# The first keys before the first norm's transposes, the first values after the first queries, and statistics next to their use, in a two-layer attention kernel

## The chip, the cores and the metric

The kernel runs on one core of a Trainium2 chip. The metric is the device time of one execution in microseconds (us); the number that counts is the median of several executions. A profile shows one of them.

A core has several engines with an instruction stream each: PE (TensorE, matmuls; "PEld" is its weight load), DVE (VectorE), ACT (ScalarE) and POOL (GpSimd). Each engine takes its instructions strictly in order, and waits where one needs a result of another engine. Transfers are started from a queue of an engine; this kernel starts nearly all of them from SP (SyncE), which does nothing else. SBUF is the memory that the engines work in; PSUM holds what matmuls write.

## The reference, cut to what matters

x has 32 sequences of 64 tokens with 512 features, and the context has the same shape. Everything is float32. Two layers follow one another; in each an attention onto the context and a feed-forward part are added to x.

```python
# layer 0
h = layernorm(x)
q = rope(h @ wq)                       # 32 heads of 128
k, v = rope(ctx @ wk), ctx @ wv        # 8 heads, each shared by 4 query heads
s = (q @ k.T) / sqrt(128)              # 64 x 64 per sequence and head
s = where(mask1 == 0, -1e9, s)         # a mask per sequence
x = x + softmax(s) @ v @ wo
x = x + swiglu_with_dequantized_weights(layernorm(x))

# layer 1
h = layernorm(x)
q, k = rmsnorm(h @ wq), rmsnorm(ctx @ wk)   # per head
v = ctx @ wv
x = x + softmax(q @ k.T / sqrt(128) + mask0) @ v @ wo   # one mask for all
x = x + memory_ffn_with_top_k(x)
```

The lines above are the order of the computation with the names shortened; the change touches the attention parts and their loads alone.

## The kernel before, in words

The 2048 tokens are worked in four chunks (`c` = 0 to 3) of 512, that is eight sequences or four tiles of 128 tokens. The attention of a layer runs over steps `(g, c)`: for each of the eight key heads `g`, the four chunks. All of x stays in SBUF (`x_sb[c]`), and so does its normed and transposed form (`xnT[c]`), which every head of the layer uses. So each chunk is normed only once per layer: chunk 0 ahead of the first step, the others during the steps of head 0.

One norm has two functions. `norm_stats` (L251) takes the statistics of the four tiles on DVE (`bn_stats` L258, `bn_aggr` L259), adds epsilon to all four variances at once (`ve`, in the profile `vea`, L262) and takes the power −1/2 on POOL (`rsa`, L247). `norm_apply` (L266) makes for each tile `xn` on DVE (L272, `xna` in the profile), transposes it by four matmuls with the identity into PSUM (L277, `xta`), and copies that to `xnT` on ACT (L281). The letter behind the names is the norm: a is layer 0's attention norm, c and d are later ones.

Queries and outputs are products of 512 by 512 that are computed as seven block products of eight matmuls (`quarters` L199, `product` L189) in place of eight. Each needs sums of blocks of both factors: `left_sums` (L163, four adds L166 to L169) on the first factor and `right_sums` (L171, four POOL adds L174 to L177) on the second. For the queries the first factor is the weight `wq` and the second `xnT`; for the output the first is the attention result `oT` and the second `wo`. The products are taken in the order P1, P2, P5, P6, P3, P7, P4; P1 and P2 use plain blocks, P5 the first sum of both sides.

A step consists of:

- `project_k` (L355, matmuls `pk` L363) and in layer 0 `rotate` (L405): ACT swaps halves (L410), DVE multiplies by cos (L412) and sin (L413), POOL adds into `kT` (L414). In layer 1 the keys are squared and summed for the norm instead.
- `project_q` (L416): the seven products; four times a "quarter" of the queries is finished by DVE (L427) and in layer 0 rotated like the keys, the last step again the POOL add (L414, `qT`).
- `norms` (L459, layer 1 alone): the sums of squares go through small matmuls (`pm` L471, L478), DVE (`qs` L484) and a power on POOL (`qr`, L247).
- `scores` (L488, matmuls `S` L496) into one PSUM buffer, and `softmax` (L505): `copy_predicated` of the mask on DVE (L519), maximum (L556), subtraction (L569), exp on ACT (L571), reciprocal (L574), multiplication on POOL (L577). DVE spreads maxima and sums by L301.
- `project_v` (L386, `pv` L395), `values` (L585, `po` L597, copied to `oT` on ACT L605, then left sums of `oT` on POOL) and the output products (`O`, L189), added to x on DVE (L242).

Work of neighbouring steps is interleaved: `run` (L660) issues the softmax of a step around the output products of the step before and the keys and queries of the step after. Before the loop `start` (L654) does the first step's left sums, keys, values and queries, in that order. `run` takes hooks, functions that are called at a given step; here `behind_first(c)` is called at step (0, c) and issues chunk c's mask flags and all of chunk c+1's norm. A framework derives the semaphores from the data, and its order on an engine is the order of issue, except that a block under `tc.issue_after(ins)` is ordered on its engine behind the instruction `ins`. `behind_first` orders its block behind the last `xn` of chunk 0.

Buffers set limits as well: `xn`, the raw masks and the spread maxima share four buffers of one kind (`m2_tile`), the rotation has two temporary buffers, and PSUM six tiles of one bank each for all products.

The loads are issued in the order of the code on SP's queue: wk and wv of head 0 (`load_kv`), the context of chunk 0 in one transfer of 1 MB (L105), wq in four pieces of 256 KB, cos, sin, a mask, x of chunk 1, wo, the other chunks of x and the constants. Only x of chunk 0 is issued on ACT's queue, at the very beginning (`load_x(0, nc.scalar)`, L110; L101 is the transfer itself).

Of the kernel before, what the change touches and what calls it, by code (L numbers as in the profile page):

```python
# [18 lines left out]
P = 128  # L19
# [25 lines left out]
def tile_xattn_ffn_2_layers(ctx: ExitStack, tc: tile.TileContext, a: dict, out: bass.AP):  # L45
# [264 lines left out]
    class Attention:  # L310
# [24 lines left out]
        def load_kv(self, g):  # L335
            kv = wkv_tile(f"wkv{self.L}_{g}").rearrange("p (k j n) -> p k j n", k=KT, j=2)
            for j, n in enumerate(self.names[1:3]):
                nc.sync.dma_start(
                    kv[:, :, j, :],
                    a[n][:, g * HD : (g + 1) * HD].rearrange("(k p) n -> p k n", p=P),  # L340
                )
            self.wkv[g] = kv
# [12 lines left out]
        def project_k(self, g, c, ctxT):  # L355
# [10 lines left out]
            if self.L == 0:  # L366
                self.rotate(
                    f"rk{n}",
                    ps,
                    lambda t: kT if t is None else t,  # L370
                    lambda t: t.rearrange("p (f w) -> p f w", f=NH),
                    lambda tab: tab.rearrange("p e j k -> p (e j k)")
                    .unsqueeze(1)
                    .to_broadcast([P, NH, 4 * S]),
                )
                return kT, None
# [28 lines left out]
        def rotate(self, name, src, dst, view, over):  # L405

            t = tmp_tile(name)
            h = HD // 2
            for lo, hi in ((0, h), (h, HD)):
                nc.scalar.copy(t[lo:hi, 1], src[HD - hi : HD - lo])  # L410
            x = t[:, 0] if src.space == bass.MemoryType.PSUM else src
            nc.vector.tensor_tensor(view(x), view(src), over(cosT), ALU.mult)  # L412
            nc.vector.tensor_tensor(view(t[:, 1]), view(t[:, 1]), over(sinT), ALU.mult)  # L413
            nc.gpsimd.tensor_tensor(dst(None), dst(x), dst(t[:, 1]), ALU.add)  # L414

        def project_q(self, g, c):  # L416
# [4 lines left out]
            )  # L421
            if self.L == 0:
                part = None

                def quarter(i, f, x, y):
# [10 lines left out]
                    )  # L436

            else:

                part = sm.tile([P, 2, NH, 2 * 4 * KH], F32, tag="part", name=f"part{n}")  # L440

                def quarter(i, f, x, y):
# [9 lines left out]
                        part[:, i, f], q2.rearrange("p (g q) -> p g q", q=KB), AX.X, ALU.add,  # L452
# [4 lines left out]
            return qT, part  # L457
# [195 lines left out]

        def start(self):  # L654
            left_sums(self.wq[0], engine=nc.vector if self.L == 0 else nc.gpsimd)
            k = self.project_k(0, 0, self.ctx)
            self.v = self.project_v(0, 0, self.ctx)
            self.state = k, self.project_q(0, 0)

        def run(self, hooks, joined, after, between=lambda c: None, tail=lambda: None, late={}):  # L660
# [13 lines left out]
            scales = self.norms(0, 0, kpart, part)  # L674
            st = self.scores(0, 0, kT, qT)
# [598 lines left out]
    norm_stats(0, "a")  # L1274
    first = norm_apply(0, "a")
    att0.start()

    def behind_first(c):
        with tc.issue_after(first):
            mask_flags(c)  # L1280
            if c == 0:
                key_weight()
            if c < last:
                load_mask(c + 1)
                norm_stats(c + 1, "a")
                norm_apply(c + 1, "a")
# [129 lines left out]
```

## Time and profile before

| what | value |
|---|---|
| three executions | 2887.97, 2888.47, 2891.56 us, median 2888.47 |
| the profiled execution | 2885.5 us |
| its span, first instruction to last | 2883.7 us |
| mean granted clock of TensorE | 0.993 |
| PE, DVE, POOL, ACT busy | 2811.7, 1886.3, 1333.8, 826.8 us |
| data moved | 130.77 MB, 45 GB/s over the span |

How to read the lines of the profile: a timeline line has the start and the length of a group of neighbouring instructions of one kind (in us), the engine, the line of the kernel, the operation, the output and the inputs by the program's names, the tile shape and the number of instructions; in brackets stands how long the engine was idle in front of it, and which engine and line released it. A line of waits has the waiting engine and what it waited for, then the total, the number and the longest wait. In a window the busy time of each engine within the stretch is followed by the clock that TensorE was granted (1.00 is full speed), the share of the DMA engines' time and the rate.

A matmul of the block products takes about 0.22 us, so a product of eight takes 1.8 and a step's 56 about 12.25 us; the values' 32 take 3.8, the scores' 32 take 1.93, the sixteen transposes of a chunk 1.9. An add of 128 x 512 on POOL takes 1.27, one on DVE 0.68.

### The profile page before, as it was taken

Reading aid. Unit: us, or ns where it says so; the run is one execution under the profiler, and the core shown is the slowest. Engines: PE = TensorE matmul, PEld = TensorE weight load, DVE = VectorE, ACT = ScalarE, POOL = GpSimd, SP = SyncE. Lnnn points to the kernel's source line nnn. Section 1 sums busy time; section 2 is a strip of 40 time slices with the busy share of each in tenths; the row PEclk is TensorE's granted clock in tenths of the full one; section 3 lists DMA queues with packets and bytes.
Section 4 is the critical chain, followed back from the end, with each engine's and each line's share of the span. In section 5 each row is a group of like instructions: output and inputs, shape, how many; then the busy total and the mean of one; then the engine's idle time right before and its main releaser. Section 6 shows DMA issues by size and latency. Waiting matters only on the chain.

```text
span 2883.7 us, 41290 instructions
## 1 busy us (share of the span) xinstructions
PE 2811.7 (98%) x16742; PEld 2265.9 (79%) x16742; DVE 1886.3 (65%) x2813; ACT 826.8 (29%) x1398; POOL 1333.8 (46%) x1032
## 2 busy tenths in 40 slices
PE   7999999999999999899999999999999999999997
PEld 5878787888888887688888677888888888888765
DVE  7677777777777776656655665555555555555566
ACT  3333333333333333211111222222222222222333
POOL 5554545454545445444443444444444444444431
PEclk9999999999999999899999999999999999999998
DMA  4111111111111110100001102020202020202001
GB/s 164 39 45 52 47 55 53 47 52 52 45 54 45 53 44 23 30 22 23 19 9 38 46 30 70 33 66 30 66 30 66 30 66 30 66 30 66 16 1 59
DMA packets 103812, 130.77 MB, mean 45 GB/s; under 512 B 8725, under 2 KB 65165, under 8 KB 103623
## 3 DMA queue, kind: packets, MB, share of 16 engines
q1 hardware_dynamic: 103047, 127.09, 13.3%
q8 instruction: 133, 2.18, 0.3%
q10 hardware_dynamic: 576, 1.05, 0.1%
q14 instruction: 56, 0.46, 0.1%
HBM read 123.92 MB, written 4.19 MB: 44 GB/s over the span
## 4 chain that ended last, share of the span: by engine, by line
PE 91%; DVE 5%; POOL 1%; ACT 1%; issue 1%; DMA 1%; SPq 0%; ACTq 0%; DVEq 0%; POOLq 0%
PE P L189 33%; PE O L189 27%; PE pv L395 8%; PE pk L363 7%; PE po L597 4%; PE S L496 4%; PE D L189 4%; ACT rq L410 1%; DVE x L242 1%; PE pqy L1105 1%; PE pu L1105 1%; DVE xnd L272 0%; PE pd L964 0%; DVE h L427 0%; DVE h L412 0%
## 5 line engine op out<-in xcount | busy, mean ns | idle before, releaser
L189 PE MATMUL O<-wo,oT 128*128 128x256 f32 x3584 | 802.5, 381 | 2.9 <-ACT oT L605 2.4
L189 PE MATMUL P<-xnT,wq 128*128 128x256 f32 x3584 | 787.8, 380 | 10.0 <-ACT h L214 9.8
L189 PEld LDWEIGHTS P<-xnT,wq 128*128 128x128 f32 x3584 | 681.2, 190 | 132.4 <-issue 31.5
L189 PEld LDWEIGHTS O<-wo,oT 128*128 128x128 f32 x3584 | 670.1, 190 | 116.5 <-issue 25.0
L242 DVE TENSOR_TENSOR x<-x,O 128x512 f32<-128x512 f32 (+1 forms) x448 | 368.5, 823 | 251.3 <-PE O L189 251.2
L577 POOL TENSOR_TENSOR s<-s,ib 128x512 f32<-128x512 f32 x128 | 169.3, 1343 | 527.3 <-DVE ib L301 505.9
L214 ACT COPY h<-P 128x512 f32<-128x512 f32 (+1 forms) x352 | 202.8, 576 | 567.3 <-PE P L189 563.5
L414 POOL TENSOR_TENSOR qT<-h,rq 128x512 f32<-128x512 f32 x128 | 175.4, 1370 | 236.4 <-DVE rq L413 236.4
L571 ACT ACTIVATE s<-s 128x1024 f32<-128x1024 f32 x64 | 67.7, 1057 | 735.1 <-DVE s L569 735.1
L247 POOL TENSOR_TENSOR qr<-qs,nhalf 128x20 f32<-128x20 f32 x32 | 113.4, 3543 | 355.2 <-DVE qs L484 354.7
L189 PE MATMUL P<-xnT,wgu 128*128 128x256 f32 (+1 forms) x1232 | 271.2, 380 | 2.5 <-DVE x L242 2.3
L189 PEld LDWEIGHTS P<-xnT,wgu 128*128 128x128 f32 (+1 forms) x1232 | 229.8, 187 | 45.7 <-DVE x L242 10.6
L395 PE MATMUL pv<-wkv,ctxT 128*128 128x128 f32 x1984 | 246.2, 280 | 1.2 <-DVE h L427 1.2
L395 PEld LDWEIGHTS pv<-wkv,ctxT 128*128 128x128 f32 x1984 | 228.5, 192 | 22.5 <-issue 18.2
L363 PE MATMUL pk<-ctxT,wkv 128*128 128x512 f32 x496 | 223.2, 592 | 0.3 <-DVE h L427 0.3
L410 ACT COPY rq<-h 64x512 f32<-64x512 f32 x256 | 157.9, 617 | 123.1 <-DVE h L427 115.1
L412 DVE TENSOR_TENSOR h<-h,cosT 128x512 f32<-128x512 f32 x128 | 91.6, 715 | 123.0 <-ACT rq L410 122.8
L363 PEld LDWEIGHTS pk<-ctxT,wkv 128*128 128x128 f32 x496 | 94.1, 190 | 93.5 <-issue 89.6
L445 DVE TENSOR_TENSOR qT<-h,P 128x512 f32<-128x512 f32 x128 | 87.9, 687 | 107.3 <-PE P L189 101.2
L451 DVE TRANSPOSE_TENSOR_REDUCE part<-q 128x16 f32<-128x512 f32 x128 | 90.6, 709 | 91.7 <-ACT q L447 87.8
L924 DVE TENSOR_TENSOR h<-h,P 128x512 f32<-128x512 f32 (+1 forms) x96 | 61.3, 641 | 134.5 <-PE P L189 101.5
L931 POOL TENSOR_TENSOR hT<-h,h 128x512 f32<-128x512 f32 (+1 forms) x48 | 56.6, 1182 | 191.7 <-DVE h L924 191.7
(253 smaller groups left out, 3453.1 us busy)
## 6 DMA issues: line engine op xcount, KB each, us to landing
ctxT<-in_ctxT SPq DMA_DIRECT2D x62, 1024.0 KB
wq<-in_L_wq SPq DMA_DIRECT2D x32, 256.0 KB
wo<-in_L_wo SPq DMA_DIRECT2D x32, 256.0 KB
wq<-in_L_wqT SPq DMA_DIRECT2D x32, 256.0 KB
wo<-in_L_woT SPq DMA_DIRECT2D x32, 256.0 KB
wgu<-in_qweight_gu SPq DMA_DIRECT2D x40, 128.0 KB
out<-o SPq DMA_DIRECT2D x16, 256.0 KB
x<-in_x SPq DMA_DIRECT2D x12, 256.0 KB
```

Of the source, the lines that this page charges most:

```text
L189: ins = nc.tensor.matmul(pv[0:w, m, :], left[:, l, k, m * P : m * P + w], right[:, r, k, :], start=(first and m == 0 and k == 0), stop=(k ...
L214: last_copy = nc.scalar.copy(t[size], ps[size]).ins
L242: return nc.vector.tensor_tensor(dst, dst, src, ALU.add).ins
L247: return nc.gpsimd.tensor_tensor(dst, src, nhalf[:, : src.shape[-1]], ALU.pow).ins
L363: nc.tensor.matmul(ps, wkv[:, k, 0, :], ctxT[:, k, :], start=(k == 0), stop=(k == KT - 1))
L395: nc.tensor.matmul(ps[:, t * HD : (t + 1) * HD], ctxT[:, k, t * P : (t + 1) * P], wkv[:, k, 1, :], start=(k == 0), stop=(k == KT - 1),)
L410: nc.scalar.copy(t[lo:hi, 1], src[HD - hi : HD - lo])
L412: nc.vector.tensor_tensor(view(x), view(src), over(cosT), ALU.mult)
L414: nc.gpsimd.tensor_tensor(dst(None), dst(x), dst(t[:, 1]), ALU.add)
L496: nc.tensor.matmul(s5[j * KB : (j + 1) * KB, f, e], kT[:, f, e, j], qT[:, f * 4 + j].rearrange("p h q -> p (h q)"), start=True, stop=True,)
L577: nc.gpsimd.tensor_tensor(sv[:, f], sv[:, f], ib[:, f * W : (f + 1) * W].unsqueeze(1).to_broadcast([P, KH, W]), ALU.mult,)
L597: nc.tensor.matmul(po[j][:, f * W : (f + 1) * W], v[rows, f, e], probs[rows, f, e], start=(e == 0), stop=(e == KH - 1),)
```

## The change

The core of it is in five parts.

1. The loads come in another order: wk, context of chunk 0 in four pieces, wv, x of chunk 0 (now on SP's queue), cos, sin, then wq and the rest as before.
2. The matmuls of the first keys are issued ahead of the first norm, and so stand on PE ahead of the norm's transposes. The rotation of these keys is ordered behind the last `xn` of that norm.
3. The first norm's statistics are finished by halves: epsilon and power after two tiles and after four.
4. `start` is split into `start_k` and `start_q`. In `start_q` the left sums come first, then the queries, then the values; before, the values stood in front of the queries. This holds for both layers, since layer 1 calls `start` too.
5. The norms of the chunks 1 to 3 are placed anew. Chunk 0's mask flags, the key weight and the statistics of chunk 1 are issued behind the left sums of wq. The statistics of chunk 2 are issued at step (0, 1) and those of chunk 3 at step (0, 2), in each case together with the step's mask flags and behind the latest multiplication by sin of the queries (`turning`). `xn` and the transposes of a chunk are ordered behind `turning` on DVE and behind the latest rotation's add on POOL (`turned`); for chunk 1 the point on DVE is the second quarter of the first queries. The hook of step (0, 0) is now run before the first scores.

Order of the instructions that results, where it differs. On PE at the start: keys, transposes of chunk 0, P, values, transposes of chunk 1, S, keys, P. At the steps (0, 1) and (0, 2): O1, O2, S of the next chunk, three tiles' transposes, one matmul of O6, the fourth tile's transposes, the rest of O6, O4. On DVE at these steps: the last multiplication by sin, mask flags, four `bn_stats`, `ve`, three `xn`, two output adds, `copy_predicated` of the new S, the fourth `xn`. On POOL: the power for the norm, then the four left sums of `oT`. In layer 1: keys, P, values, then the transposes, `pd` (a product of layer 0's feed-forward part, L964), `pm`, S, keys.

```diff
-    def load_ctx(c, name):
+    def load_ctx(c, name, pieces=1):
         t = ctx_tile(f"ctxT{name}")
-        nc.sync.dma_start(
-            t, a["ctxT"][:, c * CH : (c + 1) * CH].rearrange("(k p) t -> p k t", p=P)
-        )
+        src = a["ctxT"][:, c * CH : (c + 1) * CH].rearrange("(k p) t -> p k t", p=P)
+        for k in range(0, KT, KT // pieces):
+            part = slice(k, k + KT // pieces)
+            nc.sync.dma_start(t[:, part], src[:, part])
         return t
-
-    load_x(0, nc.scalar)
...
             if self.L == 0:
-                self.rotate(
+                with tc.issue_after(ahead()) if ahead else nullcontext():
+                    self.rotate(
...
-            nc.vector.tensor_tensor(view(t[:, 1]), view(t[:, 1]), over(sinT), ALU.mult)
-            nc.gpsimd.tensor_tensor(dst(None), dst(x), dst(t[:, 1]), ALU.add)
+            self.turning = nc.vector.tensor_tensor(
+                view(t[:, 1]), view(t[:, 1]), over(sinT), ALU.mult
+            ).ins
+            self.turned = nc.gpsimd.tensor_tensor(dst(None), dst(x), dst(t[:, 1]), ALU.add).ins
...
+                    if (i, f) == (0, 1):
+                        part()
...
+        def start_k(self, ahead=None):
+            self.k = self.project_k(0, 0, self.ctx, ahead)
+
+        def start_q(self, behind_sums=lambda ins: None, part=lambda: None):
+            behind_sums(left_sums(self.wq[0], engine=nc.vector if self.L == 0 else nc.gpsimd))
+            self.state = self.k, self.project_q(0, 0, part)
+            self.v = self.project_v(0, 0, self.ctx)
+
         def start(self):
-            left_sums(self.wq[0], engine=nc.vector if self.L == 0 else nc.gpsimd)
-            k = self.project_k(0, 0, self.ctx)
-            self.v = self.project_v(0, 0, self.ctx)
-            self.state = k, self.project_q(0, 0)
+            self.start_k()
+            self.start_q()
...
             scales = self.norms(0, 0, kpart, part)
+            for hook in hooks.pop((0, 0), ()):
+                hook()
             st = self.scores(0, 0, kT, qT)
...
-    att0.load_kv(0)
-    att0.ctx = load_ctx(0, "first")
-    att0.load_q(0)
+
+    def first_ctx():
+        att0.ctx = load_ctx(0, "first", KT)
+
+    att0.load_kv(0, first_ctx)
+    load_x(0, nc.sync)
     nc.sync.dma_start(cosT, a["cosT"])
     nc.sync.dma_start(sinT, a["sinT"])
+    att0.load_q(0)
...
-    norm_stats(0, "a")
-    first = norm_apply(0, "a")
-    att0.start()
+
+    def first_norm():
+        norm_stats(0, "a", 2)
+        return norm_apply(0, "a")
+
+    att0.start_k(first_norm)
+
+    def first_stats(c):
+        mask_flags(c)
+        if c < last:
+            load_mask(c + 1)
+            norm_stats(c + 1, "a")
+
+    def second_stats(ins):
+        with tc.issue_after(ins):
+            first_stats(0)
+            key_weight()
+
+    half = []
+    att0.start_q(second_stats, lambda: half.append(att0.turning))
 
     def behind_first(c):
-        with tc.issue_after(first):
-            mask_flags(c)
-            if c == 0:
-                key_weight()
-            if c < last:
-                load_mask(c + 1)
-                norm_stats(c + 1, "a")
-                norm_apply(c + 1, "a")
+
+        if c > 0:
+            with tc.issue_after(att0.turning):
+                first_stats(c)
+        if c < last:
+            with tc.issue_after(half[0] if c == 0 else att0.turning), tc.issue_after(att0.turned):
+                norm_apply(c + 1, "a")
```

`load_kv` takes a function that it calls between wk's and wv's transfer; `norm_stats` has had the parameter for halves (`at_once`) before.

More of the change, by code (lines that the diff above doesn't have):

```diff
@@ L1 @@
 import math
-from contextlib import ExitStack
+from contextlib import ExitStack, nullcontext
 import concourse.bass as bass
@@ L333, in load_q, with load_kv @@
             self.wq[g] = w
-        def load_kv(self, g):
+        def load_kv(self, g, between=lambda: None):
             kv = wkv_tile(f"wkv{self.L}_{g}").rearrange("p (k j n) -> p k j n", k=KT, j=2)
             for j, n in enumerate(self.names[1:3]):
+                if j == 1:
+                    between()
                 nc.sync.dma_start(
@@ L353, in load_out, with project_k @@
             self.loaded = ins.ins
-        def project_k(self, g, c, ctxT):
+        def project_k(self, g, c, ctxT, ahead=None):
             n = f"{self.L}_{g}_{c}"
@@ L366, in project_k @@
             if self.L == 0:
-                self.rotate(
[L368 to L375, printed above, removed]
+                with tc.issue_after(ahead()) if ahead else nullcontext():
+                    self.rotate(
+                        f"rk{n}",
+                        ps,
+                        lambda t: kT if t is None else t,
+                        lambda t: t.rearrange("p (f w) -> p f w", f=NH),
+                        lambda tab: tab.rearrange("p e j k -> p (e j k)")
+                        .unsqueeze(1)
+                        .to_broadcast([P, NH, 4 * S]),
+                    )
                 return kT, None
@@ L412, in rotate, with project_q @@
             nc.vector.tensor_tensor(view(x), view(src), over(cosT), ALU.mult)
-            nc.vector.tensor_tensor(view(t[:, 1]), view(t[:, 1]), over(sinT), ALU.mult)
-            nc.gpsimd.tensor_tensor(dst(None), dst(x), dst(t[:, 1]), ALU.add)
-        def project_q(self, g, c):
+            self.turning = nc.vector.tensor_tensor(
+                view(t[:, 1]), view(t[:, 1]), over(sinT), ALU.mult
+            ).ins
+            self.turned = nc.gpsimd.tensor_tensor(dst(None), dst(x), dst(t[:, 1]), ALU.add).ins
+        def project_q(self, g, c, part=lambda: None):
             n = f"{self.L}_{g}_{c}"
@@ L421, in project_q @@
             )
+            sums = None
             if self.L == 0:
-                part = None
                 def quarter(i, f, x, y):
@@ L436, in quarter @@
                     )
+                    if (i, f) == (0, 1):
+                        part()
             else:
-                part = sm.tile([P, 2, NH, 2 * 4 * KH], F32, tag="part", name=f"part{n}")
+                sums = sm.tile([P, 2, NH, 2 * 4 * KH], F32, tag="part", name=f"part{n}")
                 def quarter(i, f, x, y):
@@ L451, in quarter @@
                     nc.vector.tensor_reduce(
-                        part[:, i, f], q2.rearrange("p (g q) -> p g q", q=KB), AX.X, ALU.add,
+                        sums[:, i, f], q2.rearrange("p (g q) -> p g q", q=KB), AX.X, ALU.add,
                         apply_transpose=True,
@@ L456, in project_q @@
             quarters(n, self.wq[g], xnT[c], quarter)
-            return qT, part
+            return qT, sums
         def norms(self, g, c, kpart, part):
```

## The prediction

> **What bounds the kernel.** I read the chain that ended last first, then TensorE's waits (all idle time in front of a PE instruction, by releaser), then the windows (busy time per engine in a stretch, with the clock), then the timelines of single engines around the edits.
>
> From the page, the busy shares and the chain by engine:
>
> ```profile
> PE 2811.7 (98%) x16742; PEld 2265.9 (79%) x16742; DVE 1886.3 (65%) x2813; ACT 826.8 (29%) x1398; POOL 1333.8 (46%) x1032
> ...
> PE 91%; DVE 5%; POOL 1%; ACT 1%; issue 1%; DMA 1%; SPq 0%; ACTq 0%; DVEq 0%; POOLq 0%
> ```
>
> TensorE is busy for 98% and carries 91% of the chain. An edit that adds no matmul can therefore change the time only through the holes in PE's row. The waits that the edits touch, and the windows of the start and after it:
>
> ```profile
> PE xta L277 <- DVE xna L272: 11.8, 1, 11.8
> PE P L189 <- ACT h L214: 9.8, 5, 3.8
> PE S L496 <- POOL qT L414: 3.2, 1, 3.2
> ...
> 0.00:62.76 62.76, 45.05 (x257) 34.93 (x257) 50.45 (x91) 21.74 (x35) 35.83 (x41) 1.00 0.50 171
> 62.76:180.00 117.24, 117.24 (x732) 96.15 (x736) 81.06 (x105) 45.53 (x77) 65.77 (x50) 1.00 0.15 49
> ```
>
> Columns of the first three: total, count, longest. In the windows the length comes first, then PE, PEld, DVE, ACT, POOL. Up to the second chunk's values (62.76 us) PE is idle for 17.7 us: 11.76 before its first transpose, the rest in smaller holes. In the next 117.24 us it is never idle, and the steps of chunks 2 and 3 lie there: whatever is made late there is new idle time. PE takes its work in a fixed order, so a late transpose holds everything behind it.
>
> **The change, part by part.**
>
> **A. The start.** Keys before the norm's transposes, values behind the queries, loads in order of use and halved statistics all act here. The rows of before:
>
> ```profile
> 11.76 3.84 PE L277 MATMUL xta<-ident,xna 128*128 128x128 f32 x16 [11.76 <-DVE xna L272]
> 15.43 3.60 PE L363 MATMUL pk<-ctxTfirst,wkv 128*128 128x512 f32 x8
> 18.87 3.73 PE L395 MATMUL pv<-wkv,ctxTfirst 128*128 128x128 f32 x32
> 22.44 12.25 PE L189 MATMUL P<-xnT,wq 128*128 128x256 f32 x56
> 44.13 1.93 PE L496 MATMUL S<-qT,kT 128*32 128x256 f32 x32 [3.22 <-POOL qT L414]
> ```
>
> Loads: the last wq piece gated VectorE's first sum at 13.37, when 302 GB/s had moved 4.04 MB, of which 3.67 were ahead of it by need. Now 0.26 MB of cos and sin precede wq too, so it lands at about 14.05 (4.30 MB at 305 GB/s); x's last tile, now behind wk, context and wv on SP's queue, at about 10.2 instead of 8.79. VectorE does that wq sum (0.69) before the fourth xn (0.54), so xn ends near 15.2, its four transposes at 15.75, and P starts there instead of at 22.44: 6.7 us earlier, because keys (3.4) and values (3.6) no longer stand in front. SP's issues (about 0.45 each) and the four now missing from ACT's queue are covered by these landings.
>
> But P's end doesn't set S. P1 and P2 (16 matmuls of 0.219, to 19.25) are followed by P5, which needs the first right sum on POOL, now queued behind the key rotation's add: rotation on VectorE 15.2 to 16.5, kT on POOL 17.05 to 18.2, the sum to 19.9. P (9.4 more) ends at 28.65, pv at 32.35. POOL goes on: three xnT and four wo sums, 1.27 each but stretched where VectorE's wq sums run, to 29.9; the next rsqrt (1.02) to 30.9; then four qT adds, each behind its rotation on VectorE and, from the second on, beside xn of chunk 1: the first ends at 32.35, the last at about 40.2 (the four took 31.14 to 44.07 before, 12.9; from 30.9 with 9.3, because they no longer wait for P). xn of chunk 1 ends near 40.5, S starts at 41.0 against 44.13. From S to the second chunk's values were 18.63 us; now all of P(1) lies behind S, some 2 matmuls and the waits for h: 19.45. The values come at 60.45 instead of 62.76: **gain 2.3**. If P starts at half clock (the early transposes took 0.24 each, the later ones 0.12), it ends 1 us later and POOL covers that. Ends: with no collision between VectorE and POOL S starts at 36.9, gain 6.4; if PE is cold at S (1.9, under C) and the first exp about 1 us later, a loss of 0.6.
>
> **B. Chunks 2 and 3: their statistics move from the start into the step that uses them.** Before, xn of these chunks was ready long ahead (chunk 3's by 88.8, transposed at 109.18). Now statistics wait for the last sin product of the queries, and their rsqrt stands on POOL ahead of the four left sums of oT. One step, from the rows of chunk 3's:
>
> ```profile
> 98.15 2.01 PE L597 MATMUL po<-s,v 32*128 32x256 f32 x32
> 107.31 1.93 PE L496 MATMUL S<-qT,kT 128*32 128x256 f32 x32
> 109.18 1.97 PE L277 MATMUL xta<-ident,xna 128*128 128x128 f32 x16
> 110.98 8.80 PE L189 MATMUL O<-wo,oT 128*128 128x256 f32 x40
> ...
> 102.06 1.76 DVE L413 TENSOR_TENSOR rq<-rq,sinT 128x512 f32<-128x512 f32 x1
> 109.31 2.05 DVE L519 COPY_PREDICATED S<-minv,neg 128x1024 f32<-128x1024 uint8 x1 [1.21 <-PE S L496]
> ...
> 105.19 1.27 POOL L166 TENSOR_TENSOR oT<-oT 128x512 f32<-128x512 f32 x1
> ```
>
> Count from 98.15. VectorE is free at +5.67; mask flags 0.32 and four bn_stats with bn_aggr 2.85 (as at 16.44 to 19.26) give vea at +8.84; rsqrt on POOL (1.02) ends at +10.07. Now three xn (0.54) and POOL's left sums (1.27) start together. The rows of before show such pairs taking turns: two xn beside two POOL multiplications took
>
> ```profile
> 83.75 2.63 DVE L272 TENSOR_SCALAR xna<-x,mva,rsa 128x512 f32<-128x512 f32 x2
> 83.43 2.67 POOL L577 TENSOR_TENSOR s<-s,ib 128x512 f32<-128x512 f32 x2 [3.04 <-DVE ib L301]
> ```
>
> so 1.3 each; I take 1.45 with the hand-over, which puts the three at +11.6, +13.05, +14.5. The fourth xn stands behind two output adds (0.69 each, +15.65) and the predicated copy of S (1.1 when POOL leaves it alone, +16.75): +17.3. Its transposes end at +17.75; before, all 16 were done at +12.83. Of these 4.9 us one O matmul (0.19) fills a part: **4.7 lost**. In chunk 2's step VectorE's last sin product ends at 67.71, 4.95 after the values' start against 3.73 in chunk 3's; 0.86 of that are an xn and mask flags which leave, so 5.0 there. Together **+9.7**. Behind the stalled transposes wait O6, O4 and the next keys; nothing else is on PE to fill the hole. Ends: with no taking of turns at xn (+11.7 for the three), but the copy at its 2.05, the stall is 2.9 a step, 5.8; with full turns of 1.27 + 0.54 each, it is 5.7 a step, 11.4.
>
> The Trainium skill speaks against this part: "SBUF — State Buffer", section "Who interferes with whom", says that VectorE and GpSimd share one pair of ports as an exclusive lock, held for a whole instruction, which a tensor_scalar in its two-port mode wants too. By that rule alone each xn would wait a whole sum, the 11.4 above; the two rows with 2.63 and 2.67 say somewhat less, and the sum keeps the rows' value.
>
> **C. Layer 1's start: values behind queries.** P starts at 1618.5 instead of 1622.06. In the gap between P and the step's second product stand scores, transposes and pd; pd then starts at 1636.05 instead of 1639.03, and all that hangs on it (qs, the 3.53 us power on POOL, exp, the h copy) moves by 2.95. That chain's end is what PE waits for:
>
> ```profile
> 1645.49 3.53 POOL L247 TENSOR_TENSOR qr<-qs,nhalf 128x20 f32<-128x20 f32 x1 [0.41 <-DVE mvc L259]
> 1660.07 0.57 ACT L214 COPY h<-P 128x512 f32<-128x512 f32 x1
> 1660.69 4.05 PE L189 MATMUL P<-xnT,wq 128*128 128x256 f32 x10 [3.79 <-ACT h L214]
> ...
> 1661.00:1662.00 1.00, 1.00 (x3) 0.82 (x3) 1.00 (x3) 0.17 (x1) 0.00 (x0) 0.50 0.03 8
> ```
>
> The copy ends at 1657.7; PE, with pv now in front of pm, is ready at 1654.05 and waits 3.65 us, nearly as long as now. After the 3.79 us wait the clock column reads 0.50: ten matmuls took 4.05 instead of 2.16, so 1.9 lost. After the 3.22 us in front of S at 44.13 S took 1.93 as everywhere. At 3.65 I take the slow clock: P ends at 1662.8 instead of 1664.74, **gain 2.0**. Ends: 3.6 if the clock stays, 0 if the chain moves with something I don't see.
>
> The clock's rule in "TensorE: Matmul & The Clock Gate", section "Part 1: The HAM clock gate (the "warmup" mystery)", has a free-running window of about 3.4 us, so that the same wait may or may not be punished. By it C would be worth 2.0 or 3.6, and it agrees with the warm 3.22 and the cold 3.79 here.
>
> The rest (halved first statistics: one more tensor_scalar of 0.17 and a rsqrt of 1.02 under the loads; context in four DMAs, three more issues of 0.5 on SP while data flows) I cost at nothing: the wq landing at 14.05 covers both, and without that cover they would cost up to 1.2 and 1.5.
>
> **Sum.** −2.3 + 9.7 − 2.0 = +5.4 us. The profiled execution took 2885.5 (span 2883.7 and 1.8 around it), 3.0 under the median of the runs, 2888.47. So 2890.9 by the profile, **2893.9** as a median of runs.
>
> **Rivals.**
> 1. *Faster: xn is ready before S in B.* For it: VectorE has 65% load and the statistics themselves take only 3.2 us. If the collisions cost nothing B falls to 5.8 and A gains 6.4: 5.8 − 6.4 − 2.0 = −2.6; if the fourth xn also passes the copy, which the order on VectorE speaks against, B is near 1.4 a step and the sum −5.6: 2883 to 2886. It decides when xn3 is done within 1.6 us of S's end. Against it: the pair rows above.
> 2. *Slower: the clock falls to half after the new holes.* In A PE is idle or nearly so between 32.35 and 41, in B 4 transposes at a time with 1 us holes between. Each halving costs 1.9: with two or three 2898 to 2900. It decides where a hole passes from 3.2 to 3.8 us. Against it: B's hole is broken by transposes every 1.45 us.
> 3. *It changes nothing outside the start*: the transposes of B stall by about the gain of A and C, 4.3 in all, because O4 or keys move up. For it: nothing in the order of PE. 2888.5, give or take 2.
>
> **How the numbers follow.** Forecast (all three parts as costed, +2 to +9) 0.50; rival 1 0.19; rival 2 0.21; rival 3 0.10. A measurement of this kernel tells about 0.2%, 5.8 us, from no change; the forecast, at +5.4, is split by that bound, 0.27 same and 0.23 slower. Rival 1 gives 0.13 faster and 0.06 same, rival 2 0.21 slower, rival 3 0.10 same: 0.13, 0.43, 0.44. The range runs from 2883 (rival 1's far end, −5.6) to 2901 (rival 2 on top of the sum, +12.5, which also takes in B's 11.4); outside are A's and C's best ends together and three halvings with B's worst.
>
> **What will show it.** Right: keys from about 4 us, P from 15.8, S near 41, the second chunk's values near 60.4; PE waits for DVE's xn of 4 to 5 us twice between 65 and 120 us, with the fourth xn behind the predicated copy; layer 1's P right behind its keys and a wait for ACT's h of about 3.6. Wrong: transposes of chunks 2 and 3 that follow S without a hole (then rival 1), S earlier than 38 or later than 43 (then my POOL queue is off), half clock at S.

## The result and the profile after

The changed kernel takes 2902.28 us as a median against 2888.22 us for the kernel before, run beside it: the ratio is 1.0043, 95% interval [1.0029, 1.0058], so 8 to 17 us slower. The forecast was 2893.9, with 0.44 on slower; the range ended at 2901. The change was later run again, unedited: 1.0051 [1.0039, 1.0063]. One of the six executions of the changed kernel took 4189.9 us at a mean granted clock of 0.653; the ratio leaves it out.

The profiled execution took 2902.03 us, its span is 2900.2 us, 16.5 more than before. Of that, 3 belong to the profile of before, which was a quick one (2885.5).

From the page of the changed kernel, the busy shares and the chain by engine:

```profile
PE 2824.0 (97%) x16742; PEld 2273.3 (78%) x16742; DVE 1885.6 (65%) x2814; ACT 826.7 (29%) x1398; POOL 1333.0 (46%) x1033
...
PE 89%; DVE 6%; ACT 2%; POOL 1%; issue 1%; DMA 1%; SPq 0%; DVEq 0%; ACTq 0%; POOLq 0%
```

PE does the same 16742 matmuls, and its busy time has grown by 12.3 us. Where the same matmuls take longer and the clock column reads less than 1.00, the clock is at work; the windows below show where. It is not the clock everywhere: the first keys are counted as busy for 5.35 us instead of 3.60 while it reads 1.00, because their weight loads wait in between for the four pieces of the context. So the loss has two parts, waiting and slow matmuls. TensorE's waits (total, count, longest):

```profile
PE xta L276 <- DVE xna L271: 16.0, 12, 4.7
...
PE P L188 <- ACT h L213: 8.2, 4, 3.9
PE pk L365 <- DMA ctxTfirst<-in_ctxT: 5.0, 1, 5.0
```

The one wait for xn of before (11.8 at the start) has become twelve. To see where the time went, I put the starts of each step's values (`pv`) of both traces side by side:

| start of the values of | before | after | later by | added here |
|---|---|---|---|---|
| (0, 1) | 62.76 | 64.19 | 1.43 | 1.43 |
| (0, 2) | 100.09 | 109.91 | 9.82 | 8.39 |
| (0, 3) | 137.17 | 151.57 | 14.40 | 4.58 |
| (1, 0) | 172.54 | 186.95 | 14.41 | 0.01 |
| (1, 1) | 210.51 | 226.57 | 16.06 | 1.65 |
| layer 0, (7, 3) | 1144.46 | 1161.12 | 16.66 | 0.60 |
| layer 1, (0, 1) | 1666.91 | 1683.35 | 16.44 | −0.22 |

The rows (0, 2) and (0, 3) end the stretches in which chunks 2 and 3 are normed, part B of the prediction; they are called chunk 2's and chunk 3's step below. The windows of the changed kernel show the clock there (length, then PE, PEld, DVE, ACT, POOL busy, the granted clock, DMA share, GB/s):

```profile
0.00:64.19 64.19, 48.87 (x257) 36.33 (x257) 42.71 (x71) 21.79 (x36) 35.95 (x40) 0.92 0.50 167
...
0.00:5.00 5.00, 0.00 (x0) 0.00 (x1) 0.15 (x1) 1.28 (x1) 1.44 (x15) 1.00 0.56 135
...
73.00:83.00 10.00, 6.26 (x34) 4.27 (x24) 9.41 (x11) 2.34 (x4) 6.14 (x6) 0.68 0.01 4
83.00:92.36 9.36, 9.36 (x36) 7.88 (x35) 6.31 (x9) 1.06 (x1) 4.56 (x5) 0.80 0.03 12
...
116.00:127.00 11.00, 7.24 (x62) 4.76 (x61) 9.59 (x14) 2.34 (x4) 6.73 (x6) 1.00 0.21 80
```

In the kernel before the clock reads 1.00 from 62.76 to 180; here it is 0.92 over the start and 0.68 and 0.80 in chunk 2's step. In the first 5 us 135 GB/s flow here, and 198 in the kernel before:

```profile
0.00:5.00 5.00, 0.00 (x0) 0.00 (x0) 0.88 (x2) 1.28 (x1) 1.00 (x11) 1.00 0.65 198
```

The timeline of PE in the two steps:

```profile
71.55 1.93 PE L503 MATMUL S<-qT,kT 128*32 128x256 f32 x32
74.94 0.63 PE L276 MATMUL xta<-ident,xna 128*128 128x128 f32 x4 [1.45 <-DVE xna L271]
76.34 0.94 PE L276 MATMUL xta<-ident,xna 128*128 128x128 f32 x4 [0.78 <-DVE xna L271]
77.75 1.08 PE L276 MATMUL xta<-ident,xna 128*128 128x128 f32 x4 [0.47 <-DVE xna L271]
78.63 1.06 PE L188 MATMUL O<-wo,oT 128*128 128x256 f32 x2
80.73 1.09 PE L276 MATMUL xta<-ident,xna 128*128 128x128 f32 x4 [1.04 <-DVE xna L271]
81.61 10.91 PE L188 MATMUL O<-wo,oT 128*128 128x256 f32 x38
...
117.14 1.93 PE L503 MATMUL S<-qT,kT 128*32 128x256 f32 x32
119.56 0.63 PE L276 MATMUL xta<-ident,xna 128*128 128x128 f32 x4 [0.49 <-DVE xna L271]
120.97 0.63 PE L276 MATMUL xta<-ident,xna 128*128 128x128 f32 x4 [0.78 <-DVE xna L271]
122.37 0.63 PE L276 MATMUL xta<-ident,xna 128*128 128x128 f32 x4 [0.78 <-DVE xna L271]
125.35 0.63 PE L276 MATMUL xta<-ident,xna 128*128 128x128 f32 x4 [1.71 <-DVE xna L271]
```

The same four transposes take 0.63 at full clock and 1.08 at half. In chunk 2's step the holes add up to 3.74 us, and behind them 38 O matmuls took 10.91 us where 40 took 8.80 before. Chunk 3's step has holes of the same sum, 3.76 us, at full clock. What TensorE waits for there, on VectorE and GpSimd:

```profile
116.62 0.17 DVE L261 TENSOR_SCALAR vea<-mva 128x4 f32<-128x4 f32 x1
116.87 1.02 POOL L246 TENSOR_TENSOR rsa<-vea,nhalf 128x4 f32<-128x4 f32 x1 [1.81 <-DVE vea L261]
117.92 4.30 DVE L271 TENSOR_SCALAR xna<-x,mva,rsa 128x512 f32<-128x512 f32 x3 [1.13 <-POOL rsa L246]
122.15 1.46 DVE L241 TENSOR_TENSOR x<-x,O 128x512 f32<-128x512 f32 x2
123.53 1.23 DVE L526 COPY_PREDICATED S<-minv,neg 128x1024 f32<-128x1024 uint8 x1
124.67 0.54 DVE L271 TENSOR_SCALAR xna<-x,mva,rsa 128x512 f32<-128x512 f32 x1
```

The start, with the sum of wq on VectorE that waits for the load, and layer 1's start:

```profile
5.03 5.35 PE L365 MATMUL pk<-ctxTfirst,wkv 128*128 128x512 f32 x8 [5.03 <-DMA ctxTfirst<-in_ctxT]
15.04 3.63 PE L276 MATMUL xta<-ident,xna 128*128 128x128 f32 x16 [4.67 <-DVE xna L271]
16.41 0.69 DVE L165 TENSOR_TENSOR wq<-wq 128x512 f32<-128x512 f32 x1 [0.29 <-DMA wq<-in_L_wq]
18.51 3.62 PE L188 MATMUL P<-xnT,wq 128*128 128x256 f32 x16
23.17 8.90 PE L188 MATMUL P<-xnT,wq 128*128 128x256 f32 x40 [1.04 <-POOL xnT L173]
...
43.62 2.98 PE L503 MATMUL S<-qT,kT 128*32 128x256 f32 x32
...
1632.30 3.60 PE L365 MATMUL pk<-ctxTsecond,wkv 128*128 128x512 f32 x8
...
1674.88 6.61 PE L188 MATMUL P<-xnT,wq 128*128 128x256 f32 x16 [3.86 <-ACT h L213]
```

P starts 3.9 us earlier than before, the scores 0.5 earlier, and they take 2.98 instead of 1.93. In layer 1 sixteen matmuls stand behind the wait for h, at about half clock.

### The profile page after: what moved, and what is told of

The parts are those of the page before. It is cut to its first block, busy times and chain, and to the rows that moved or that the text cites. A ratio compares the mean times of both kernels' runs of the same rounds, so it can differ in the third digit from the quotient of the medians.

```text
span 2900.2 us, 41308 instructions
## 1 busy us (share of the span) xinstructions
PE 2824.0 (97%) x16742; PEld 2273.3 (78%) x16742; DVE 1885.6 (65%) x2814; ACT 826.7 (29%) x1398; POOL 1333.0 (46%) x1033
## 4 chain that ended last, share of the span: by engine, by line
PE 89%; DVE 6%; ACT 2%; POOL 1%; issue 1%; DMA 1%; SPq 0%; DVEq 0%; ACTq 0%; POOLq 0%
PE P L188 33%; PE O L188 26%; PE pv L398 8%; PE pk L365 7%; PE po L604 4%; PE S L503 4%; PE D L188 3%; ACT rq L413 1%; DVE x L241 1%; PE pqy L1120 1%; DVE rq L416 1%; DVE h L415 1%; PE pu L1120 1%; DVE xna L271 0%; DVE h L432 0%
```

## The experiments

Every edit is on the changed kernel unless it says otherwise. Times are medians in us, ratios are against the kernel before, run beside each, with their 95% intervals.

| kernel | median | ratio |
|---|---|---|
| the change, twice | 2902.28, 2904.14 | 1.0043 [1.0029, 1.0058], 1.0051 [1.0039, 1.0063] |
| norms of chunks 2, 3 early | 2892.51 | 1.0010 [1.0000, 1.0019] |
| layer 1: values first | 2900.38 | 1.0038 [1.0023, 1.0053] |
| x on ACT's queue | 2899.43 | 1.0033 [1.0021, 1.0046] |
| added transposes | 2897.63 | 1.0033 [1.0018, 1.0047] |
| wo sums late | 2899.28 | 1.0038 [1.0024, 1.0052] |
| P4 before P7 | 2902.51 | 1.0047 [1.0033, 1.0061] |
| statistics a step earlier | 2894.10 | 1.0021 [1.0011, 1.0030] |
| four edits | 2892.64 | 1.0012 [1.0002, 1.0022] |
| five edits | 2889.24 | 1.0008 [0.9999, 1.0017] |
| two edits on the kernel before | 2896.10 | 1.0024 [1.0014, 1.0035] |
| five edits, xn of chunk 2 moved | 2890.04 | 1.0003 [0.9994, 1.0012] |

### The norms of chunks 2 and 3 early again

```diff
...
-        if c > 0:
-            with tc.issue_after(att0.turning):
-                first_stats(c)
-        if c < last:
-            with tc.issue_after(half[0] if c == 0 else att0.turning), tc.issue_after(att0.turned):
-                norm_apply(c + 1, "a")
+        if c > 0:
+            with tc.issue_after(first[0]):
+                first_stats(c)
+                if c < last:
+                    norm_apply(c + 1, "a")
+        else:
+            with tc.issue_after(half[0]), tc.issue_after(att0.turned):
+                norm_apply(1, "a")
```

`first[0]` is the last xn of chunk 0.

> The changed kernel, with the norms of the chunks 2 and 3 (statistics, xn and mask flags) queued behind the first norm's last xn again, as before; everything else of the change stays. Theory (the late statistics cost the two steps 8.4 and 4.6 us of TensorE's time, waits and slow clock together): about 13 us faster than the changed kernel, 2889 by the median; TensorE's waits for xn in these two steps gone, the values of the third and fourth chunk 37.3 and 37.1 us behind the ones before them, as in the kernel before. Rival (the statistics only move the loss: in the start they stand in front of the rotations on VectorE and GpSimd): the first scores come 3 us later or more, and the gain is under 9.

The ratio falls from 1.0043 to 1.0010, with intervals that don't touch: some 10 us. The steps of chunks 2 and 3 take 37.32 and 37.08 us from values to values, as in the kernel before (37.33 and 37.08). PE's timeline of this kernel, chunk 2's step:

```profile
74.45 1.93 PE L503 MATMUL S<-qT,kT 128*32 128x256 f32 x32
76.31 1.97 PE L276 MATMUL xta<-ident,xna 128*128 128x128 f32 x16
78.12 8.80 PE L188 MATMUL O<-wo,oT 128*128 128x256 f32 x40
```

The transposes follow the scores without a hole. But the second chunk's values start at 66.98, 2.8 later than in the changed kernel: the early statistics go in front of the rotations, the first scores come at 44.74 instead of 43.62, and waits and slow matmuls follow. The gain was 13 in the two steps and 10 in all. So the late norms are the cause of most of the loss, and the rival was right that a part of it moves to the start, though less than it said (1.1 us at the scores, not 3).

### Transposes that do nothing, in the holes

```diff
             pt = mm_tile(f"xt{name}{c}_{t}")
+            if name == "a" and c > 0:
+                for _ in range(6):
+                    nc.tensor.transpose(pt[:, 0:P], ident, ident)
```

> The changed kernel, with six more transposes of the identity ahead of each tile's transposes for the chunks 1 to 3 (72 matmuls, about 8.7 us of TensorE's work at full clock, results overwritten). They stand in the holes in which TensorE waits for xn. Theory (the holes bring the half clock, which costs 1 us at the first scores and 3.4 of the 8.4 us in chunk 2's step): the clock stays at 1.00 from 73 to 93 us, and the kernel is 3 to 4.5 us faster although it does more. Rival (the loss is waiting alone): 0 to 3 us slower, since some of the added matmuls stick out of the holes.

The kernel with 72 matmuls more is 4.7 us faster by the medians; the intervals overlap, so the time alone doesn't decide. The windows of this kernel in chunk 2's step do (columns as above):

```profile
73.00:83.00 10.00, 7.78 (x50) 6.68 (x51) 9.26 (x11) 2.77 (x5) 6.59 (x6) 1.00 0.04 13
83.00:93.00 10.00, 10.00 (x40) 7.18 (x39) 6.29 (x9) 1.59 (x3) 5.10 (x5) 1.00 0.00 0
```

The clock stays at 1.00, the first scores take 1.93 us, the O products 8.85 for 40, and chunk 2's step costs 5.7 us more than before in place of 8.4. Chunk 3's costs 5.0 in place of 4.6, since some of the added matmuls stick out. So of the 8.4 us that chunk 2's step cost in the first profile some 2.7 were the clock and the rest waiting.

### Statistics one step earlier

```diff
-        if c > 0:
-            with tc.issue_after(att0.turning):
-                first_stats(c)
         if c < last:
             with tc.issue_after(half[0] if c == 0 else att0.turning), tc.issue_after(att0.turned):
                 norm_apply(c + 1, "a")
+            with tc.issue_after(att0.turning):
+                first_stats(c + 1)
```

> The changed kernel, with the statistics of the chunks 2 and 3 one step earlier: behind the last multiplication by sin of the step before, so that only xn stands in the step that uses it. The start up to the first scores is that of the changed kernel. Theory: xn of these chunks is ready when the scores end, the transposes follow without a hole; steps of 37.3 and 35.4 us from values to values as in the kernel without the late statistics, 10 to 13 us faster than the changed kernel, and 2 to 3 faster than with the norms queued early in the start, which made the first scores later. Rival (VectorE is late in any case): waits for xn of 1 to 3 us a step remain.

Chunk 3's step is as before (0.4 more). Chunk 2's still costs 5.3 more, and for a new reason, which PE's timeline of this kernel shows:

```profile
73.82 1.53 PE L276 MATMUL xta<-ident,xna 128*128 128x128 f32 x12
75.57 0.63 PE L276 MATMUL xta<-ident,xna 128*128 128x128 f32 x4 [0.21 <-DVE xna L271]
79.20 10.59 PE L188 MATMUL O<-wo,oT 128*128 128x256 f32 x40 [3.00 <-DVE x L241]
```

xn is in time, but now the statistics of chunk 3 stand on VectorE ahead of the output adds, and O6, which goes on into the PSUM tile that an add must have read, waits 3.00 us; the clock falls, and 40 O matmuls take 10.59. Neither theory had seen this wait. In neither of the two places tried between the last rotation and the scores' mask, ahead of xn or behind three of them, had VectorE room for 3 us of statistics.

### The loads: x on ACT's queue

```diff
+    load_x(0, nc.scalar)
...
     att0.load_kv(0, first_ctx)
-    load_x(0, nc.sync)
```

> The changed kernel, with x of chunk 0 issued on ACT's queue at the very start again. Theory (one queue with its transfers in a row moves only 135 GB/s in the first 5 us where two moved 198, so that wq lands at 16.4 instead of 14.1): x's tiles come from 4 us on, wq lands near 14, the queries start 2 us earlier or more, the first scores 1 to 2.4 us earlier, total 1 to 2.4 us faster than the changed kernel. Rival (GpSimd's queue sets the scores, the loads only the start of P): P earlier, but the first scores within 0.5 us of 43.6 and the time unchanged.

188 GB/s instead of 135 flow in the first 5 us, x's first tile is there at 3.89 instead of 10.53, P starts at 15.14 instead of 18.51, the scores at 42.36 instead of 43.62. So the loads account for 1.3 us of the scores' start, and the theory held; of that 0.8 reaches the second values, because the scores themselves took 3.40 us at about half clock. The time is not told apart from the change's.

### GpSimd's sums of wo behind the first queries

```diff
                     if c == 0:
-                        right_sums(self.wo[g])
+                        with tc.issue_after(self.turned) if g == 0 and self.L == 0 else nullcontext():
+                            right_sums(self.wo[g])
```

> The changed kernel, with GpSimd's four sums of the first wo (5.9 us from 26.9 to 32.7, first needed at the first output products near 72 us) queued behind the last add into the first queries. Theory (GpSimd's queue sets the start of the first scores): the queries' adds move up by what they wait for the wo sums, the first scores start 2 us earlier or more (at 41.5 or before against 43.6) and the total falls by 1 to 3. Rival (VectorE's rotations and their collisions set it): the scores within 0.7 us of 43.6.

The scores start at 41.13 instead of 43.62, the second values at 62.65 instead of 64.19. In the changed kernel it is thus GpSimd's queue that holds back the scores, as the prediction had it. A part is given back: the first value products now wait 0.7 us for GpSimd's multiplication of the probabilities, behind the moved sums. The time is again not told apart.

### Layer 1: values first again

```diff
+            if self.L == 1:
+                self.v = self.project_v(0, 0, self.ctx)
             self.state = self.k, self.project_q(0, 0, part)
-            self.v = self.project_v(0, 0, self.ctx)
+            if self.L == 0:
+                self.v = self.project_v(0, 0, self.ctx)
```

> The changed kernel, with the values ahead of the queries in layer 1's start alone. By the prediction the order of the change is worth 2.0 us, so this would be 2 slower than the changed kernel. By the trace after, it is worth 0.5 to 0.8, since the wait for ACT's copy of h is as long as before (3.86 against 3.79) and more matmuls stand behind it: 0.5 to 0.8 slower. If the wait's clock depends on chance it may go either way by 3.

The medians differ by less than their intervals. The traces say more: from the first keys of layer 1 to the first value products (`po`) it takes 49.6 us in the kernel before and 49.8 here, with the values first. With the queries first it takes 49.1 and 48.8 in the two profiles of the change, 49.2 with the early norms, 47.9 with x on ACT's queue, with the wo sums late and with the statistics a step earlier, and 47.7 with the added transposes. Where the order is the same, the difference is the clock of the sixteen matmuls behind the wait: 5.2 to 6.7 us. So against the 49.8 the order gains 0.6 to 2.1 us, and which it is changes from one profile to the next.

### P4 ahead of P7 where TensorE waits for h

```diff
+        ahead = mul(4) if n in ("0_1_1", "1_0_1") else None
         mul(7, x)
         u3 = copy(3, x)
         done(1, 1, p5, x)
-        done(1, 0, u3, mul(4))
+        done(1, 0, u3, ahead if ahead is not None else mul(4))
```

> The changed kernel, with product P4 ahead of P7 in two of the 64 projections: step (0, 1) of layer 1, where TensorE waits 3.86 us for ACT's copy of h with P7 and P4 behind it, and step (1, 1) of layer 0, where it waits 2.29. P4 needs no copy and fills 1.75 us of each wait. Theory (a wait costs its length and, from somewhere between 2 and 4 us on, the half clock behind it): the waits fall to 2.1 and 0.6, the eight products behind them run at full clock; 1.75 + 3.1 in layer 1 and 1.75 + 0 to 1.7 in layer 0, together 5 to 8 us faster than the changed kernel. Rival (the slow clock comes from something else): 3.5 faster.

In the profile the waits fell as expected and the eight matmuls behind them run at full clock (PE's timeline of this kernel):

```profile
220.08 1.99 PE L188 MATMUL P<-xnT,wq 128*128 128x256 f32 x8 [0.56 <-ACT h L213]
...
1672.04 1.99 PE L188 MATMUL P<-xnT,wq 128*128 128x256 f32 x8 [2.04 <-ACT h L213]
1676.22 2.38 PE L605 MATMUL po<-s,v 32*128 32x256 f32 x32 [2.20 <-POOL s L585]
```

Against the change it gained 2.7 us at step (1, 1) and 2.4 in layer 1, where the first value products now wait 2.20 for the probabilities: 5.1 together, the low end of the theory. But the profiled execution was the fastest of four (2896.3; the others 2902 to 2905), and the median shows nothing of it: inconclusive by the time.

### Combinations

The four edits together:

> Four edits on the changed kernel together: statistics a step earlier, x of chunk 0 on ACT's queue, the wo sums behind the first queries, P4 ahead of P7 in the two projections. If the losses are separate: −11 −1 −2 −6, 20 us under the changed kernel, 2882, which is 6 under the kernel before. If the start is bound by something else, 2886.

Measured: 1.0012. The scores start at 39.64, 4.0 earlier than in the change: the two edits of the start (1.3 and 2.5) add up. But chunk 2's step keeps the 3.00 us wait of O6. Against the change 20 us were expected and some 10 came. What fell short were the two largest terms: taken alone, the statistics a step earlier brought 6 us by the ratios, not 11, and P4 ahead of P7 nothing, not 6. The four ratios taken alone add up to 9.5 us and the four together to 9.0; with intervals of 3 to 4 us on each side, the times can't tell whether the gains add up.

Five edits: the wo sums behind the first probabilities, the added transposes for chunk 1 alone, and the norms placed by hand:

```diff
+        elif c == 1:
+            with tc.issue_after(half[1]):
+                mask_flags(1)
+                norm_stats(2, "a")
+                norm_apply(2, "a")
+        elif c == 2:
+            mask_flags(2)
+            norm_apply(3, "a")
...
+            (0, 1): [lambda: load_mask(2), lambda: norm_stats(3, "a")],
```

`half[1]` is the last sin product of the first queries, and the last line is one of the hooks that are ordered behind the output adds.

> The changed kernel's start with what the runs so far pointed to: x of chunk 0 on ACT's queue, the wo sums behind the first probabilities on GpSimd, six transposes of the identity ahead of each of chunk 1's tiles, statistics of chunk 2 behind the first queries and those of chunk 3 behind the output adds of step (0, 1), P4 ahead of P7 in the two projections. Theory (late statistics, GpSimd's queue in the start, loads on one queue and the clock are the four losses): second values at 58 to 61 us against 62.8 in the kernel before, steps of chunks 2 and 3 as before, waits of the two projections down to 0.6 and 2.1: 3 to 7 us faster than the kernel before. Rival (a gain in the start is given back at the next wait): within 2 us of the kernel before.

And with xn of chunk 2 behind its own step's queries:

```diff
-            half.append(att0.turning)
+            with tc.issue_after(att0.turning):
+                mask_flags(1)
+                norm_stats(2, "a")
         elif c == 1:
-            with tc.issue_after(half[1]):
-                mask_flags(1)
-                norm_stats(2, "a")
+            with tc.issue_after(att0.turning):
                 norm_apply(2, "a")
```

The statistics of chunk 2 stay behind the first queries; only its xn moves.

> The previous combination with xn of chunk 2 moved behind the queries of its own step, out of the first softmax (where it ran beside GpSimd's multiplication of the first probabilities). Theory (the 2.15 us wait in front of the second half of the first value products is that collision): the second values at 60 to 62 us instead of 64.8, the transposes of chunk 2 still follow their scores within 0.5 us, 2 to 4 us faster than the previous combination. Rival: the wait stays, or xn is late and the transposes of chunk 2 wait 1 us or more.

Both are clearly faster than the change (1.0008 and 1.0003) and neither beats the kernel before. With the five edits the second values came at 64.79, not at 58 to 61; with xn of chunk 2 moved they came at 60.97, as that theory had it, and chunk 2's transposes followed their scores at once, but the time isn't told apart from the five edits'. The last kernel shows why. Its scores start 3.9 us earlier than in the kernel before, its second values 1.8 earlier, and its third values 2.6 later. From PE's timeline of that kernel, with one row of ACT's:

```profile
40.19 1.93 PE L508 MATMUL S<-qT,kT 128*32 128x256 f32 x32
...
60.97 3.84 PE L403 MATMUL pv<-wkv,ctxT 128*128 128x128 f32 x32 [1.19 <-DVE h L437]
...
62.71 2.52 ACT L418 COPY rq<-h 64x512 f32<-64x512 f32 x4 [4.55 <-POOL qT L424]
66.37 3.84 PE L189 MATMUL O<-wo,oT 128*128 128x256 f32 x16 [1.56 <-ACT oT L617]
...
97.13 3.69 PE L189 MATMUL P<-xnT,wq 128*128 128x256 f32 x16 [1.47 <-ACT h L214]
```

With TensorE earlier, it waits for VectorE's h, and for ACT's oT, whose copies stand behind copies that waited 4.55 us for GpSimd's queries: VectorE and GpSimd, which have the norms to do in the same 100 us, become what holds it. The rival of the five edits (a gain in the start is given back at the next wait) held.

### Two of the edits on the kernel before

The edits of the wo sums (behind the first probabilities) and of P4, on the kernel before:

> The kernel before with two of these edits alone: the wo sums behind the first probabilities on GpSimd, and P4 ahead of P7 in the two projections. Theory: the first scores 2 to 4 us earlier than 44.1, and the waits for ACT's h at step (1, 1) of layer 0 and (0, 1) of layer 1 shorter by 1.75 and about 0.5: 2 to 5 us faster than the kernel before. Rival: the first exp or VectorE's queue takes the gain back, within 1 us.

It is slower, 1.0024 [1.0014, 1.0035]. Theory and rival both fell: the scores waited the same 3.22 us for GpSimd's queries as in the kernel before. There GpSimd had idle time between the queries' adds (1.13 and 3.69 us), so the wo sums were not what they waited for. Behind the first probabilities they stand ahead of the second queries, and in this profile TensorE waits 1.68 us for h where it waited 0.60, and 1.42 for oT where it had no wait. P4 ahead of P7 made step (1, 1) 1.1 us shorter. The profiled execution was the slowest of twelve (2901.1 against a median of 2896.1). The line of the scores in PE's timeline:

```profile
45.09 3.32 PE L497 MATMUL S<-qT,kT 128*32 128x256 f32 x32 [3.22 <-POOL qT L415]
```

This line has a second use. The wait is the 3.22 us of the kernel before, in the same place, but there the scores behind it took 1.93, here 3.32.

### The change again

> The changed kernel without an edit, to have its time beside the same runs of the kernel before. Theory (a part of the difference is chance of TensorE's clock, drawn anew in every execution): the same program gives 2896 to 2906, with the mean granted clock between 0.986 and 0.990 and the lower clock in the longer executions; in its profile the waits are those of the first profile, while the places at half clock differ. Rival (the places are fixed by the program): 2901 to 2904 and the same places.

Five executions between 2901.6 and 2905.6, a ratio of 1.0051. The waits are nearly the same (3.88 us in chunk 2's step and 3.57 in chunk 3's, against 3.74 and 3.76), the clock is not: in chunk 3's step the window that read 1.00 in the first profile reads 0.82 in the second:

```profile
116.00:127.00 11.00, 7.43 (x57) 4.73 (x57) 9.59 (x14) 2.35 (x4) 6.62 (x6) 0.82 0.17 65
```

The step costs 6.9 us more than before instead of 4.6, chunk 2's 7.0 instead of 8.4. So the places are partly drawn anew, as the theory had it, while the time varies less than it expected; its range is nearer to the rival's.

## Why the prediction was right or wrong

**Direction and mechanism: right.** Slower, through the late statistics of B. **Size: too small**, +5.4 against +14 by the medians. The terms that were wrong are the landing of wq in A and the half clock, which the sum put at nothing in A and in B and too low in C.

**A, expected −2.3, measured +1.43.** The step that failed first is "it lands at about 14.05": wq's sum started at 16.41. I had kept the rate of before (305 GB/s) for a single queue; the first 16.41 us moved 276 GB/s, and the first 5 us 135. With x back on ACT's queue the scores moved 1.3 us. The rest of the chain held in its order and nearly in its length: from P's start to the scores 25.1 us against 25.25 forecast. But the landing is not the whole of it, and two of the prediction's own signs of being wrong came (scores later than 43, half clock at S). In the run with x on ACT's queue P started at 15.14 and GpSimd's last add into the queries ended at 40.06, as forecast (40.2), and still the scores came at 42.36, not 41.0: the clock read 0.50 from 39.00 to 42.40, and the last eight transposes ahead of the scores took 1.94 us, where four take 0.63 at full clock. So the landing accounts for 1.3 of the 2.6 us by which the scores were late. Then the scores ran at about half clock, 1.05 us more, a cost that I had named only for the bad end.

**B, expected +9.7, measured +13.0 (8.39 and 4.58).** Chunk 3's step went as worked out, nearly to the tenth. Counted from the start of its value products (107.97): vea at +8.82 (forecast 8.84), the rsqrt to +9.92 (10.07), three xn to +14.25 (14.5), the adds to +15.64 (15.65), the copy to +16.79 (16.75), the fourth xn to +17.24 (17.3). The loss was 4.58 against 4.7; xn took turns with GpSimd's sums, three in 4.30 us. So close a hit is in part luck. The two adds were written down 1.15 us apart where 0.69 each makes 1.38, which the earlier xn made good, and two O matmuls, not one, ran ahead of the fourth tile's transposes. Above all, this profile is one of two among six in which the step kept its full clock: with B as in the change and no transposes added, chunk 3's step cost 4.6 us twice and 6.7 to 7.0 four times, chunk 2's 6.7 to 8.4, and both together 13.0 to 15.0. In chunk 2's step the waits are the same, 3.74, and the term that failed is the clock, which the sum had at nothing. Rival 2's halving, too, costs more than the 1.9 us I gave it, because it lasts on into the O products; the added transposes take 2.7 us of it away.

**C, expected −2.0, measured −0.5 in the first profile** (from layer 1's first keys to its first value products, 49.1 us against 49.6). The copy came 3.16 us earlier (forecast 2.95) and the wait was 3.86 (3.65). But the sixteen matmuls behind it took 6.61 us, not 5.1: the half clock cost 2.9 more than the 3.72 of full clock, not 1.4. Across the profiles the order is worth 0.6 to 2.1.

**What no step held:** 1.65 us at step (1, 1), where the wait for h is as before (2.29 against 2.33) but the sixteen products behind it took 5.41 instead of 3.72, and 0.6 later in layer 0. The cause of both is open.

**The rivals.** Rival 1 did not come: the third xn ended 3.2 us behind the scores' end, not within 1.6, the fourth 6.1, and the pair rows held. Rival 2 gave the time (2898 to 2900) closest to the measured one; it came true in A and in chunk 2's step. I argued against it that "B's hole is broken by transposes every 1.45 us": that is the sentence that was wrong. Four transposes of 0.6 us in 1.4 us did not keep the clock. Rival 3 (nothing outside the start) is excluded by the table of steps.

## What to carry to other kernels

Work that is taken off a path by doing it early should not be moved to the step that uses it because the start looks crowded: an engine with 65% load may have no room at all in the stretch between two dependent operations, and 3 us of statistics in each of two steps cost 13 together here. Where the bounding engine is held by its clock as well as by its queue, price a new hole twice, once for its length and once for what runs behind it, and see whether the next independent product fits into it (empty work kept the clock here, too). And a gain at the start is worth only what the next wait leaves of it.

## What the runs showed of the hardware that was not expected

- **The same wait is punished or not.** 3.22 us in front of the first scores: 1.93 us behind it in the kernel before, 3.32 in that kernel with two edits. 2.33 and 2.29 us at step (1, 1): 3.72 and 5.41. At that step it doesn't look like chance: a wait of 2.28 to 2.31 us was followed by 5.41 in seven profiles of the changed kernel and its variants, and by 3.72 in one, that with the added transposes. What decides is open. The Trainium skill, "TensorE: Matmul & The Clock Gate", section "Part 1: The HAM clock gate (the "warmup" mystery)", has a free-running window of about 3.4 us, by which equal waits may fare differently; but the punished waits of 2.29 and 3.22 us are shorter than that window.
- **Sparse matmuls don't always keep the clock.** With four transposes of 0.63 us every 1.4 us it read 0.68 over 10 us in chunk 2's step; in chunk 3's the same pattern gave 1.00 in one profile and 0.82 in the other. With six more transposes in each hole it read 1.00 in both steps, in one profile.
- **The times go with the clock.** In 79 executions of the kernel before, run beside the experiments, between 2883.3 and 2897.0 us, the time follows the mean granted clock: 2884.5 at 0.993, 2888.2 at 0.991, 2893.7 at 0.989, about 2.1 us for 0.001. The change has 0.987 on average against 0.991; by that slope some 8 of its 14 us lie in the clock, an estimate, since the waits lower it too.
